# Layer-norm statistics combined by ScalarE and VectorE on 32 partitions instead of by TensorE, in a fused gated cross-attention and feed-forward block

## The chip, the cores and the metric

The kernel runs on one core of one Trainium2 chip. A core has five engines that work side by side, each on its own queue of instructions, in order: PE (TensorE, matmuls; its weight loads are shown as PEld), DVE (VectorE), ACT (ScalarE), POOL (GpSimd) and SP (SyncE, which issues DMAs here). On-chip data lie in SBUF, 128 partitions wide; PE writes its results to PSUM, from where DVE and ACT take them ("evict" them). The metric is the device time of one execution in microseconds; lower is better. Before the change it is 1263.37 us, the median of 3 runs (1262.82 to 1263.95).

## The reference

x is 4 x 2048 x 512, the context 4 x 77 x 384, all in float32. Sixteen heads of width 64. Layer norm has neither gain nor offset.

```python
def _layernorm(x, axis=-1, eps=1e-05):
    m = jnp.mean(x, axis=axis, keepdims=True)
    v = jnp.var(x, axis=axis, keepdims=True)
    return (x - m) / jnp.sqrt(v + eps)
...
    def _L0_xattn_ref(x, context, Wq, Wk, Wv, Wo, bo):
...
        q = split_heads(x @ Wq)
        k = split_heads(context @ Wk)
        v = split_heads(context @ Wv)
        sim = jnp.einsum('bhid,bhjd->bhij', q, k) * SCALE
        attn = jax.nn.softmax(sim, axis=-1)
        out = jnp.einsum('bhij,bhjd->bhid', attn, v)
...
        return out @ Wo + bo

    def _L0_ffn_ref(x, W, b, logits, u):
...
        gumbel = -jnp.log(-jnp.log(u))
        idx = jnp.argmax(jax.nn.log_softmax(logits) + gumbel)
        out = jnp.einsum('btd,de->bte', x, W[idx]) + b[idx]
        return out
    x = x + jnp.tanh(g_xattn[0]) * _L0_xattn_ref(_layernorm(x, axis=-1), ctx_768, ...)
    x = x + jnp.tanh(g_ffn[0]) * _L0_ffn_ref(_layernorm(x, axis=-1), ...)
    return x
```

## The kernel before

**Weights folded into the keys and values.** Since the context is short (77 keys, padded to 80), the kernel multiplies the query weights into the keys once per batch element (`m`, from `build_m`) and the output weights into the values (`vo`, from `build_vo`, which evicts six products per head pair p, by DVE or ACT after a string such as "AAD", and stores them to HBM; `load_vo` and `load_m` fetch what a batch element needs). Scores are then x times `m`, and the attention's output is the probabilities times `vo`. The centring of the layer norm is folded into the weights, so that only its factor, one over the standard deviation, has to be found for each token.

**Tiles.** The 8192 tokens are cut into 16 groups of 512. A group's rows lie in SBUF as 128 partitions x 16 x 128: partition 32a + c holds, for 16 tokens (one for each g), the a-th quarter of their 512 features. A token's statistics are therefore spread over four partitions, 32 apart. `x_columns` transposes the rows to columns for PE.

**Seven products instead of eight.** `Seven` multiplies two by two blocks by a scheme of seven products (the Strassen-Winograd sums T1 to T4 are computed by POOL in `Columns.sum`). `product(s)` issues the matmuls of step s; `post(s)` evicts what is finished: ACT copies a result to `snap`, or DVE adds one to it. Some later products accumulate in a PSUM bank that an earlier `post` must have emptied. There are seven such banks (`bank`), and an eighth, `stat`, is shared by the statistics and by `head_max`.

**Softmax.** `s_rows` (DVE) transposes scores to rows of tokens, `head_max` finds a maximum for each head quarter, `exps` (ACT) computes 64 rows of exponentials per group with the factor `up` and the offset `nmx`, `head_sum` (DVE) sums and inverts, `head_scale` (POOL) multiplies, `p_columns` (DVE) transposes the probabilities back for PE as `pT`.

**Order.** The order of the instructions on every engine is written out by hand (`manual_schedule`): an engine takes its instructions as the program emits them, and semaphores hold it where data are missing. One turn of the main loop, for group i, holds the scores of group i (ps_s, three `Seven`s: s0, then s1 and s2 together), the attention output of group j = i - 1 (ps_a) and its feed-forward product (ps_f), and the residual end of group f = i - 2 (`f_rows`, `f_scale` by ACT, `add_bias` and `f_add` by POOL, `store` by SP). Ahead of the loop, the scores of groups 0 and 1 are interleaved with `build_vo`; behind it stands the rows' end, the rest of groups 14 and 15, where work is cut into halves of 8 token rows.

**The statistics** (`Norms`, lines 361 to 422). A turn treats two norms at once: that of the feed-forward of group f (16 columns, flag `y`) and that of the next scores (16 columns, flag `x`), so n = 32; at the start and the end n is 16 or 8. `stats` runs bn_stats (DVE) for every g: it gives two means and two sums of squares for even and odd features, on each of the four partitions. `mean` adds the two means (L379), and `flush` (L384) multiplies by the constant `jm`, 128 x 128, which is 0.125 where two partitions agree modulo 32: PE thus sums over the four partitions and writes the result back to all of them. `spread` computes the deviations from PSUM (L399, L401, L403), `var` sums again and uses PE again, `rstd` adds epsilon (L412) and raises to the power -0.5 on POOL (L415, L422), 16 columns at a time; `up` and `down` (L418, L419) scale the factor for the exponentials. In the main loop `mean` stands behind s0's last `post`, and the other three steps at s = 1, 2, 3 of the loop over s1 and s2. At the start and the end, with `apart` set, the matmul is emitted one step behind the sums.

**The start and the rows' end.** At the start, `early_step` places norms[0] and norms[1] in the loop over s1 of group 0 (lines 710 to 732). In the loop over s0 of group 1 (756 to 769), `build_vo(4)` to `build_vo(7)` are interleaved with the first 57 rows of exponentials of group 0; the last seven follow at line 770, ahead of the loop over s1 and s2. At the rows' end, group 15's feed-forward is finished in halves: `half_bias` adds the bias, `scaled` (ACT) and line 1063 (DVE) apply the factor, `added` (DVE) adds, and two `store` calls write the halves, by SP and by ACT's queue.

Of the kernel before, what the change touches and what calls it, by code (L numbers as in the profile page):

```python
# [19 lines left out]
def flamingo_block_kernel(  # L20
# [82 lines left out]
    jm = cp.tile([P, NA, 32], F32, tag="jm")  # L103
# [85 lines left out]
    nc.gpsimd.memset(jm, 0.0)  # L189
    for a in range(NA):  # L190

        for a2 in range(NA):
            nc.gpsimd.affine_select(
                out=jm[:, a, :], in_=jm[:, a, :], compare_op=ALU.not_equal, fill=0.125,
                base=-32 * a2, pattern=[[-1, 32]], channel_multiplier=1)
# [165 lines left out]
    class Norms:  # L361


        apart, waiting = False, None

# [11 lines left out]
        def total(self, pairs, half):  # L377
            t = small.tile([P, self.n], F32, tag=f"tot{half}", name="tot")
            nc.vector.tensor_reduce(t, pairs, AX.X, ALU.add)  # L379
            self.waiting = half, t  # L380

        def flush(self):
            half, t = self.waiting
            nc.tensor.matmul(self.ps[:, half], jm.rearrange("p a c -> p (a c)"), t, start=True, stop=True)  # L384

        def mean(self):
            n = self.n
            self.ps = stat[:, : 2 * n].rearrange("p (h n) -> p h n", h=2)
            self.mm = self.s6.rearrange("p g (h s) -> p g h s", h=2)
            self.total(self.mm[:, :, :, 1], 0)  # L390
            if not self.apart:
                self.flush()

        def spread(self):
            n = self.n
            sq = stat[:, ds(4 * NG, 2 * n)].rearrange("p (n h) -> p n h", h=2)
            dv = small.tile([P, n, 2], F32, tag="dv", name="dv")
            for t in (dv, sq):
                nc.vector.tensor_tensor(t, self.mm[:, :, :, 1],  # L399
                                        self.ps[:, 0].unsqueeze(2).to_broadcast([P, n, 2]), ALU.subtract)  # L400
            nc.vector.tensor_tensor(sq, sq, dv, ALU.mult)  # L401
            self.q = small.tile([P, n, 2], F32, tag="q", name="q")
            nc.vector.scalar_tensor_tensor(self.q, self.mm[:, :, :, 2], 1.0 / 64, sq, ALU.mult, ALU.add)  # L403

        def var(self):
            self.total(self.q, 1)
            if not self.apart:
                self.flush()

        def rstd(self):  # L410
            self.rs = small.tile([P, self.n], F32, tag="rs", name="rs")
            nc.vector.tensor_scalar(self.rs, self.ps[:, 1], EPS, None, ALU.add)  # L412
            if self.x:
                r = self.rs[:, ds(self.x0, NG)]
                nc.gpsimd.tensor_tensor(r, r, neghalf, ALU.pow)  # L415
                self.up = small.tile([P, NG], F32, tag="up", name="up")
                self.down = small.tile([P, NG], F32, tag="down", name="down")
                nc.gpsimd.tensor_scalar(self.down, r, -SCALE, None, ALU.mult)  # L418
                nc.gpsimd.tensor_scalar(self.up, r, SCALE, None, ALU.mult)  # L419
            if self.y:  # L420
                r = self.rs[:, : min(self.n, NG)]
                nc.gpsimd.tensor_tensor(r, r, neghalf[:, : min(self.n, NG)], ALU.pow)  # L422
# [117 lines left out]
    def head_max(i, h):  # L540
        mx = stat[:, ds((8 + h) * NG, NG)]
# [132 lines left out]
    def norm_step(n, s):  # L674
        if s < 4:
            (n.mean, n.spread, n.var, n.rstd)[s]()

    def early_step(n, s):

        if s == 0:  # L680
            n.apart = True
            n.mean()
        elif s == 1:
            n.flush()
            n.spread()
            n.var()
        elif s == 2:
            n.flush()
            n.rstd()
# [20 lines left out]
    for s in range(7):  # L710
        s1.product(s)
        if s == 0:
# [3 lines left out]
            early_step(n, 0)  # L716
# [3 lines left out]
        elif s < 3:  # L720
            early_step(n, s)
            n1.stats(xg[1], 0, 8 * (s - 1), 8)
        elif s < 6:
            early_step(n1, s - 3)
        if 0 < s:
            s1.post(s)
        if s == 4:
# [8 lines left out]
    for s in range(7):  # L736
        s2.product(s)
        s2.post(s)
        if s == 5:
# [16 lines left out]
    for s in range(6):  # L756
        s0.product(s)
        s0.post(s)
        if s < 4:
            build_vo(4 + s, "DDA" if s < 2 else "D")  # L760
# [9 lines left out]
    exps(0, 57, 64)  # L770
    for s in range(7):
        s1.product(s)
        s2.product(s)
        if s == 0:
            s1.post(0)
            s2.post(0)
            s0.product(6)
# [24 lines left out]
    for i in range(1, NGRP):  # L802
# [4 lines left out]
        if 1 < i:  # L807

            s0 = scores0(i)
            for s in range(6):  # L810
# [18 lines left out]
                if s == 3 and 0 <= f:  # L829
                    add_bias(f, nc.gpsimd)  # L830
            for k in range(2):
# [4 lines left out]
            for s in range(7):  # L836
                s1.product(s)
                s2.product(s)
                if s == 0:
# [4 lines left out]
                    n.mean()  # L844
                    for k in range(2):
                        s_rows(i, KH + k, s0.chunk(1, k))
                elif s < 4:
                    norm_step(n, s)
# [111 lines left out]
    for s in range(7):  # L960
# [9 lines left out]
        if s == 1:  # L970
            n.apart = True
            n.mean()
            add_bias(f, nc.vector)
        if s == 2:
            n.flush()
            n.spread()
            n.var()
            pT[j].sum("T4")
        if s == 3:
            n.flush()  # L980
            n.rstd()
# [12 lines left out]
        if s == 6:  # L994
# [4 lines left out]
            n1.apart = n0.apart = True  # L999
            n1.mean()  # L1000
# [19 lines left out]
    def added(h, v):  # L1020
        y = by_feature(ys[j], h, v)
        nc.vector.tensor_tensor(y, y, by_feature(ts_[j], h, v), ALU.add)

    for s in range(6):
        ff.product(s)
        if s == 0:
            n1.flush()
            n1.spread()
            n1.var()
            y_rows(j, 2, 0)  # L1030
            n0.stats(ys[j], 0, 0, 8)
        if s == 1:
            n1.flush()
            n1.rstd()
            yc[j].sum("T4")
            n0.mean()
            half_bias(1, nc.vector)
        if s == 2:
            n0.flush()
            half_bias(0, nc.gpsimd)  # L1040
            n0.spread()
# [66 lines left out]
```

## Time and profile before

| | before |
|---|---|
| runs, median | 1263.37 us (1262.82 to 1263.95) |
| profiled execution, its own time | 1261.51 us |
| its span | 1259.6 us |
| TensorE clock granted, mean | 0.998 |
| matmul passes of the 128 x 256 kind, each | 379 ns from start to end, one every 0.216 us |
| statistics matmuls (L384) | 38, recorded as 76 passes |
| pow on POOL, 128 x 16 (L415) | 16, 3135 ns in the mean |
| ACT idle, mean over the periods of the main loop | 36 of 73 us |

The span is from the first to the last instruction that the profiler recorded; the execution's own time holds what lies around it too. An fp32 matmul is recorded as two passes. In a timeline, a line gives the start in us, the length in us (of the whole run of like instructions), the engine, the line of the kernel, the operation, the tile written and those read, the shapes, how many there were, and in brackets the idle time before it and what ended it. The engines' busy times overlap: they are not a sum. A line number such as L504 can be that of a helper that many places call.

### The profile page before, as it was taken

How to read it: one execution, taken by the hardware profiler on the slowest of the kernel's cores; microseconds unless marked ns; L12 is line 12 of the kernel's file. 1: busy time of each engine (PE TensorE's matmuls, PEld its weight loads, DVE VectorE, ACT ScalarE, POOL GpSimd, SP SyncE). 2: the span in 40 equal slices, each digit the busy share in tenths (PEclk: the TensorE clock that was granted, in tenths of full speed). 3: DMA queues.
4: the chain of work that ended last, by engine and by line, in shares of the span. 5: the costliest groups of instructions: out<-in, count | busy, mean ns of one | idle time of the engine just before them, and what ended most of it. 6: DMA issues, size and time to landing. Idle time of an engine off the chain costs nothing.

```text
span 1259.6 us, 16932 instructions
## 1 busy us (share of the span) xinstructions
PE 1246.9 (99%) x5780; PEld 1067.7 (85%) x5780; DVE 886.2 (70%) x1858; ACT 639.1 (51%) x1748; POOL 879.0 (70%) x483
## 2 busy tenths in 40 slices
PE   9999999999999999999999999999999999999996
PEld 6575888888888888888888888888888888888885
DVE  5789876667777676777766767766766787666566
ACT  3539453719265372926446292744628273563813
POOL 5352895866957786676968687675976697575764
PEclk9999999999999999999999999999999999999999
DMA  9766400314014030303106030212304120010102
GB/s 271 291 199 214 114 1 1 68 42 109 1 28 124 1 67 1 68 22 98 32 1 151 1 68 1 46 22 84 67 1 110 42 56 11 2 34 1 34 1 67
DMA packets 95221, 80.28 MB, mean 64 GB/s; under 512 B 3856, under 2 KB 83088, under 8 KB 95136
## 3 DMA queue, kind: packets, MB, share of 16 engines
q1 hardware_dynamic: 92768, 76.74, 24.0%
q10 hardware_dynamic: 1760, 1.34, 0.3%
q8 instruction: 46, 0.75, 0.3%
q0 software_dynamic: 608, 1.13, 0.2%
q14 instruction: 39, 0.32, 0.1%
HBM read 44.07 MB, written 35.13 MB: 63 GB/s over the span
## 4 chain that ended last, share of the span: by engine, by line
PE 96%; DVE 2%; ACT 1%; issue 0%; POOL 0%; DVEq 0%; ACTq 0%
PE ps_s L479 38%; PE ps_a L479 37%; PE ps_f L479 15%; PE ps_kv L274 2%; PE ps_vo L339 2%; PE ps_m L304 2%; PE ps_st L384 0%; ACT t L604 0%; PE ps_w L168 0%; ACT t L1018 0%; DVE s L375 0%; DVE snap L504 0%; POOL rs L422 0%; DVE vo L342 0%; DVE y L430 0%
## 5 line engine op out<-in xcount | busy, mean ns | idle before, releaser
L479 PE MATMUL ps_a<-pT,vo 128*128 128x256 f32 x2240 | 486.7, 379 | 0.0
L479 PEld LDWEIGHTS ps_a<-pT,vo 128*128 128x128 f32 x2240 | 425.5, 190 | 57.8
L550 ACT ACTIVATE s<-s,nmx,up 128x77 f32<-128x77 f32 x1024 | 355.6, 446 | 0.4 <-DVE nmx L544 0.3
L479 PE MATMUL ps_s<-tq,m 128*128 128x256 f32 x1280 | 294.2, 381 | 0.2 <-ACT snap L485 0.2
L450 POOL TENSOR_TENSOR pT<-pT 128x1280 f32<-128x1280 f32 x64 | 185.8, 2904 | 125.3 <-PE ps_a L479 111.7
L479 PEld LDWEIGHTS ps_s<-tq,m 128*128 128x128 f32 x1280 | 241.3, 190 | 35.8 <-issue 3.2
L485 ACT COPY snap<-ps_s 128x512 f32<-128x512 f32 (+1 forms) x188 | 93.8, 511 | 306.8 <-DVE t L430 131.4
L479 PE MATMUL ps_s<-xc,m 128*128 128x256 f32 x960 | 222.7, 381 | 0.0
L479 PEld LDWEIGHTS ps_s<-xc,m 128*128 128x128 f32 x960 | 180.8, 190 | 28.2 <-DVE vo L342 2.4
L561 POOL TENSOR_TENSOR s<-s,sm 128x1232 f32<-128x1232 f32 x64 | 145.1, 2268 | 65.9 <-DVE sm L558 46.1
L504 DVE TENSOR_TENSOR snap<-snap,ps_s 128x512 f32<-128x512 f32 (+1 forms) x141 | 83.5, 593 | 82.0 <-PE ps_s L479 82.0
L533 DVE STREAM_TRANSPOSE s<-snap 128x512 f32<-128x512 f32 x156 | 99.9, 685 | 46.8 <-ACT snap L485 44.8
L604 ACT ACTIVATE t<-t,rs 128x128 f32<-128x128 f32 x240 | 73.3, 389 | 100.7 <-POOL rs L422 100.7
L479 PE MATMUL ps_f<-tq,wf 128*128 128x256 f32 x512 | 118.7, 379 | 0.0
L570 DVE STREAM_TRANSPOSE pT<-s 128x512 f32<-128x512 f32 x160 | 101.0, 677 | 17.1 <-POOL s L561 17.1
L415 POOL TENSOR_TENSOR rs<-rs,neghalf 128x16 f32<-128x16 f32 x16 | 50.2, 3135 | 87.9 <-DVE rs L412 87.9
L450 POOL TENSOR_TENSOR tq<-xc,tq 128x512 f32<-128x512 f32 x64 | 85.2, 1332 | 34.9 <-PE ps_f L479 32.4
L479 PEld LDWEIGHTS ps_f<-tq,wf 128*128 128x128 f32 x512 | 97.0, 190 | 13.1
L557 DVE TENSOR_REDUCE sm<-s 128x16 f32<-128x1232 f32 x64 | 91.4, 1429 | 20.5 <-ACT s L550 20.5
L542 DVE TENSOR_REDUCE ps_st<-s 128x16 f32<-128x1232 f32 x64 | 92.4, 1444 | 2.1
L479 PE MATMUL ps_f<-xc,wf 128*128 128x256 f32 x384 | 90.8, 379 | 0.0
L450 POOL TENSOR_TENSOR tq<-xc 128x512 f32<-128x512 f32 x64 | 81.4, 1271 | 10.7 <-DVE xc L425 9.4
(126 smaller groups left out, 1137.7 us busy)
## 6 DMA issues: line engine op xcount, KB each, us to landing
xg<-in_x_dram SPq DMA_DIRECT2D x64, 256.0 KB, 5.8
out_dram<-y SPq DMA_DIRECT2D x60, 256.0 KB, 4.3
vo<-vo_d SPq DMA_DIRECT2D x16, 640.0 KB, 6.5
vo_d<-vo SPq DMA_DIRECT2D x16, 512.0 KB, 4.3
m<-m_d SPq DMA_DIRECT2D x12, 640.0 KB, 4.2
m_d<-vo SPq DMA_DIRECT2D x4, 960.0 KB, 7.9
wq<-in_WqT_dram SPq DMA_DIRECT2D x8, 256.0 KB, 6.5
wq<-in_Wo_dram SPq DMA_DIRECT2D x1, 2048.0 KB, 13.8
```

Of the source, the lines that this page charges most:

```text
L415: nc.gpsimd.tensor_tensor(r, r, neghalf, ALU.pow)
L450: (engine or nc.gpsimd).tensor_tensor(self.at[name], self.at[a], self.at[b_], op)
L479: nc.tensor.matmul(self.ps[r][:, n, :], self.w(blk, c, pair), self.cols(cname, c), start=(first and n == 0 and c == 0), stop=(c == h - 1), ...
L485: nc.scalar.copy(dst, self.ps[r])
L504: nc.vector.tensor_tensor(c, c, self.ps[r], ALU.add)
L533: nc.vector.transpose(key_chunk(sc[i], k), cols.rearrange("p (g h r) -> p g h r", h=HA, r=R))
L542: nc.vector.tensor_reduce(mx, head(i, h), AX.X, ALU.max)
L550: nc.scalar.activation(head(i, h)[:, g, :], head(i, h)[:, g, :], AF.Exp, scale=norms[i].up[:, g : g + 1], bias=nmx[h][:, g : g + 1])
L557: nc.vector.tensor_reduce(sm, head(i, h), AX.X, ALU.add)
L561: nc.gpsimd.tensor_tensor(head(i, h), head(i, h), sums[h].unsqueeze(2).to_broadcast([P, NG, J]), ALU.mult)
L570: nc.vector.transpose(pT[i].all[:, k, :].rearrange("p (g h r) -> p g h r", h=HA, r=R), key_chunk(sc[i], k))
L604: nc.scalar.activation(ts_[f][:, g, :], ts_[f][:, g, :], AF.Copy, scale=rs[:, g : g + 1])
```

## The change

In the place of `mean`, `spread`, `var`, `rstd` and the constant `jm` there are four other steps, and no matmul. `gather`: eight ACT copies bring the two means and the two sums of squares of the four partition quarters side by side on 32 partitions, the means to PSUM (`stat`), the sums to SBUF. `calc`: seven DVE operations on 32 partitions x n x 8 give the variance. `power`: POOL raises to -0.5, on 32 partitions, 16 columns at a time. `back`: four copies (by ACT, once by DVE) bring the factor to all 128 partitions; POOL then computes `down` and `up`. `head_max` moves to another part of `stat`.

Where the steps stand: in the main loop `gather` behind s0's loop, ahead of the first evictions of s1 and s2, `calc` and `power` at s = 0, `back` at s = 3. At the start, norms[0] takes s = 0, 1 and 3 of the loop over s1, and norms[1] s = 3 of that loop (`gather`) and s = 0 and 3 of the loop over s2. In the loop with `build_vo`, `build_vo(7)` is evicted as "DDA" instead of "D", so that its third and sixth product go to ACT. The last seven exponentials of group 0 come behind the first evictions of s1 and s2. At the rows' end both bias halves go to POOL, the scaling of the quarter (0, 0) and two of the four additions too, and the half that is stored first is finished after the last product instead of before it.

```diff
     class Norms:
...
-        def mean(self):
...
-        def spread(self):
...
-        def var(self):
...
-        def rstd(self):
+        def gather(self):
+
+            self.mean = stat[:32, : 8 * self.n].rearrange("p (n e) -> p n e", e=2 * NA)
+            self.m2 = small.tile([32, self.n, 2 * NA], F32, tag="m2", name="m2")
+            parts = self.s6.rearrange("p g (h s) -> p g h s", h=2)
+            for a in range(NA):
+                for to, k in ((self.mean, 1), (self.m2, 2)):
+                    nc.scalar.copy(to[:, :, ts(a, 2)], parts[ts(a, 32), :, :, k])
+
+        def calc(self):
...
+            tot, dv, self.r = tile_of([], "tot"), tile_of([2 * NA], "dv"), tile_of([], "r32")
+            nc.vector.tensor_reduce(tot, self.mean, AX.X, ALU.add)
+            wide = tot.unsqueeze(2).to_broadcast([32, self.n, 2 * NA])
+            for to in (dv, self.mean):
+                nc.vector.scalar_tensor_tensor(to, wide, -0.125, self.mean, ALU.mult, ALU.add)
+            nc.vector.tensor_tensor(self.mean, self.mean, dv, ALU.mult)
+            nc.vector.scalar_tensor_tensor(dv, self.m2, 1.0 / 64, self.mean, ALU.mult, ALU.add)
+            nc.vector.tensor_reduce(tot, dv, AX.X, ALU.add)
+            nc.vector.tensor_scalar(self.r, tot, 0.125, EPS, ALU.mult, ALU.add)
+
+        def power(self):
+            for at in range(0, self.n, NG):
+                r = self.r[:, at : min(at + NG, self.n)]
+                nc.gpsimd.tensor_tensor(r, r, neghalf[:32, : r.shape[1]], ALU.pow)
+
+        def back(self, copy=nc.scalar.copy):
             self.rs = small.tile([P, self.n], F32, tag="rs", name="rs")
+            for a in range(NA):
+                copy(self.rs[ts(a, 32)], self.r)
             if self.x:
                 r = self.rs[:, ds(self.x0, NG)]
-                nc.gpsimd.tensor_tensor(r, r, neghalf, ALU.pow)
...
     def norm_step(n, s):
-        if s < 4:
-            (n.mean, n.spread, n.var, n.rstd)[s]()
...
         if s == 0:
+            n.gather()
         elif s == 1:
+            n.calc()
+            n.power()
         elif s == 2:
+            n.back()
...
+        if s == 0:
+            norm_step(n1, 1)
+        if s == 3:
+            norm_step(n1, 2)
...
         if s < 4:
-            build_vo(4 + s, "DDA" if s < 2 else "D")
+            build_vo(4 + s, "D" if s == 2 else "DDA")
...
-    exps(0, 57, 64)
     for s in range(7):
         s1.product(s)
         s2.product(s)
         if s == 0:
             s1.post(0)
             s2.post(0)
+            exps(0, 57, 64)
             s0.product(6)
             s0.post(6)
...
+            n.gather()
             for k in range(2):
                 s_rows(i, k, s0.chunk(0, k))
...
                     s0.product(6)
                     s0.post(6)
-                    n.mean()
+                    n.calc()
+                    n.power()
                     for k in range(2):
                         s_rows(i, KH + k, s0.chunk(1, k))
-                elif s < 4:
-                    norm_step(n, s)
+                elif s == 3:
+                    n.back()
...
     for s in range(6):
         ff.product(s)
         if s == 0:
+            half_bias(1, nc.gpsimd)
+            n1.calc()
+            n1.power()
             y_rows(j, 2, 0)
             n0.stats(ys[j], 0, 0, 8)
             yc[j].sum("T4")
+            half_bias(0, nc.gpsimd)
+        ff.post(s)
         if s == 2:
+            n1.back()
+            n0.gather()
         if s == 3:
             f_rows(j, ff, 0, 1)
             scaled(0, 1, n1.rs)
+            n0.calc()
+            n0.power()
         if s == 4:
             f_rows(j, ff, 1, 1)
             scaled(1, 1, n1.rs)
+            added(0, 1, nc.gpsimd)
         if s == 5:
             f_rows(j, ff, 0, 0)
+            n0.back(nc.vector.tensor_copy)
+            scaled_at_once(0, 0, n0.rs, nc.gpsimd)
+            added(0, 0, nc.gpsimd)
     ff.product(6)
     for k in range(2):
         to_rows(ts_[j], ff.ps[0][:, k, :], 2 + k, 0)
+    added(1, 1, nc.vector)
+    store(j, 8, 8, (nc.sync, nc.sync, nc.sync, nc.scalar))
+    scaled_at_once(1, 0, n0.rs, nc.vector)
+    added(1, 0, nc.vector)
     store(j, 0, 8, (nc.sync, nc.scalar))
```

## The prediction

> **What bounds the kernel now.** I read the busy shares first, then the chain that ended last, then TensorE's timeline in one period of the main loop, then the timelines of all engines at the start and at the end.
>
> ```profile
> PE 1246.9 (99%) x5780; PEld 1067.7 (85%) x5780; DVE 886.2 (70%) x1858; ACT 639.1 (51%) x1748; POOL 879.0 (70%) x483
> PE 96%; DVE 2%; ACT 1%; issue 0%; POOL 0%; DVEq 0%; ACTq 0%
> ```
>
> PE is 99% busy and makes 96% of the chain: what leaves PE leaves the time, and what the other engines do is free until PE waits for it. That gives three questions: what the removed matmuls cost on PE, where the new work makes PE wait, and what becomes of the stretch after PE's last matmul.
>
> ```profile
> 488.80 1.89 PE L479 MATMUL ps_s<-tq,m 128*128 128x256 f32 x8
> 490.52 0.30 PE L384 MATMUL ps_st<-tot,jm 128*128 128x32 f32 x2
> 490.67 5.43 PE L479 MATMUL ps_s<-tq,m 128*128 128x256 f32 x24
> 495.93 0.30 PE L384 MATMUL ps_st<-tot,jm 128*128 128x32 f32 x2
> 496.07 2.84 PE L479 MATMUL ps_s<-xc,m 128*128 128x256 f32 x12
> ```
>
> A line is start, length, group. An fp32 matmul is two passes; in the chain 140 ps_a passes take 30.22 us, 0.2159 each. The first statistics matmul holds PE from 490.52 to 490.67 (0.15), and the 24 passes behind it take 5.26 where 24 x 0.2159 is 5.18 (0.08 more): 0.23 each, and PE waits for nothing here.
>
> **Part 1: the statistics matmuls of the main loop go.** The 14 periods from the first ps_a of one group to that of the next (141.72 to 1163.60) sum to 1021.88 us. A period holds 168 tiled matmuls, 336 passes, 72.53 us; 14 of them 1015.4. So 6.5 us are something else; three periods are 0.12 longer than the others for a reason of their own, which I leave in. Gain **6.1 us**, bounds 4.1 (28 x 0.145, the visible slots alone) and 6.5.
>
> The work that takes their place must hide. One group, in times of before:
> - gather, eight ACT copies: the last bn_stats ends at 485.2, so about 485.2 to 486.6. ACT is idle from 481.8 to 488.5, where s1's first eviction starts.
> - calc, seven VectorE operations, now on 32x256 instead of 128x64: 128x256 rows take 0.42 (L504) to 0.48 (L583), together some 2.7. VectorE is idle from 488.56 to 491.40, so it ends near 491.1; the s_rows behind it wait for ACT until 491.4 anyway.
> - power, two pows of 2.9 (L415) on POOL, idle from 489.8: 491.1 to 497.0, where it was 496.5 to 502.9.
> - back, four ACT copies behind evictions that end at 496.5: 497.0 to 497.7; POOL's down and up to 498.3. Behind them stand f_scale (ready 5 us earlier than before), ACT's evictions at 505.9, and on POOL T2 of pT at 511. None is reached.
>
> So nothing is lost there. If the cover were gone, PE would first feel it at s1's T2 product (493), which needs the eviction behind gather: it has 4 us to spare.
>
> **Part 2: prices of the small operations.** ACT copies of 16 to 64 elements out of SBUF are not in the trace. In the nearest rows, 128x8 and 128x80, ACT starts one 0.12 after the other (48.40, 48.52), or 0.22 where it needs the result (48.18, 48.40). Each PSUM copy of gather waits for the one before: four pairs of 0.24 and a tail, **1.2 us**; back 4 x 0.12 and a tail, **0.6**. Upper bounds at f_scale's pitch (3.03 for 10): 2.4 and 1.2. I take the lower, whose sizes are nearer. calc on 32x128 lies between 128x64 (0.23) and 128x256 (0.42): **2.0**, bounds 1.3 and 2.7. pow with 16 columns: **2.9** as L415, whose columns are the same; bounds 1.65 (L422, 8 columns, the faster) and 4.1 (the longest L415).
>
> The rows just named price the small ACT operation at 0.12 to 0.22. [...]
>
> **Part 3: the start, where cover ends.**
>
> ```profile
> 116.49 1.72 PE L339 MATMUL ps_vo<-wq,wf 64*64 64x512 f32 x4 [0.55 <-DVE snap L504]
> 111.37 13.82 ACT L550 ACTIVATE s<-s,nmx,up 128x77 f32<-128x77 f32 x40
> 128.42 2.26 POOL L561 TENSOR_TENSOR s<-s,sm 128x1232 f32<-128x1232 f32 x1
> 130.72 4.27 DVE L570 STREAM_TRANSPOSE pT<-s 128x512 f32<-128x512 f32 x7 [3.78 <-POOL s L561]
> 137.62 0.64 DVE L504 TENSOR_TENSOR sn<-sn,ps_s 128x512 f32<-128x512 f32 x1
> ```
>
> Lines of PE, ACT, POOL and DVE: ACT computes exponentials without a gap to 125.2; VectorE sums the last head, POOL scales it (to 130.7), VectorE transposes p_columns, and only then adds the score quarter (137.62 to 138.26) that PE's last s1 product needs at 138.97. The slack is 0.7 us, and the change puts work into this chain at two places.
>
> First, norms[1]. Its gather is covered (ACT waits until 85.8 for wfr anyway). Its calc stands on VectorE behind four s_rows: 90.7 to 92.7; pow to 95.6; back to 96.2. ACT's last s2 eviction, now behind back, ends at 96.6 instead of 94.9, and head_max starts at 97.3 instead of 95.7. VectorE is 1.6 late, but had waited 0.57 and 0.67 for PE in this stretch: 0.4 remain. ACT is 0.9 late.
>
> Second, the shifted evictions. Before, ACT had 32 exponentials done at 114.1; now at 115.0 it finds the third and the sixth eviction of build_vo(7). The sixth product is not there before 118.2: PE gets its bank only when VectorE has evicted another, as the first line shows. ACT stands still, evicts, and is free at 118.9. 25 exponentials x 0.345 reach 127.5, the two evictions moved ahead 128.4, the last seven 130.9: 5.7 later. Sum (1.7) and scale (2.26) end at 134.9 instead of 130.7; POOL's own queue had hidden 1.5. All of VectorE's p_columns move by 4.2, the needed add ends at 142.5, and PE, due at 138.97, loses 3.5. The next exponentials start 0.7 later against PE, whose T1 of yc had 0.4 of slack (ready 173.25, needed 173.67): 0.2 more. That swallows what leaves PE before (four statistics matmuls, waits of 0.20 and 0.71). Loss **3.7 us**. Lower bound 3.3 (ACT waits for the sixth product even if norms[1] costs nothing); upper 8.2, with the upper prices of part 2 in all six steps (ACT and VectorE then carry norms[0] late into norms[1] too). jm's 16 selects (0.21 each) leave POOL before 10 us, where PE waits for no POOL: 0.
>
> **Part 4: the rows' end.**
>
> ```profile
> 1231.58 2.29 DVE L608 TENSOR_TENSOR y<-y,t 128x2048 f32<-128x2048 f32 x1 [2.92 <-ACT t L604]
> 1252.95 1.29 DVE L1022 TENSOR_TENSOR y<-y,t 128x512 f32<-128x512 f32 x2
> 1254.28 0.89 ACTq L612 DMA_DIRECT2D out_dram<-y  x2
> ```
>
> The second to last group's pow is free to start when POOL's T4 ends (1221.7, not 1223.8): back at 1225.2, 16 f_scale to 1230.0, f_add to 1232.3 instead of 1233.9. Everything queued behind that add on VectorE is 1.5 earlier: n1's stats end at 1235.9, gather 1237.1, calc 1238.8, n0's stats 1241.1. PE loses six statistics matmuls and a wait of 0.34 and ends near 1248.1, not 1250.2. Then in a row on VectorE: back to 1249.0, two transposes to 1249.8, three adds and scalings of 0.65 to 1251.8. POOL's half: pow to 1248.4, add, scale, add of 1.27 each (L576) to 1252.2. The last store is issued at 1252.1 instead of 1254.3; its issue count per queue and its 5.3 us to the end stay. Gain **2.2**, bounds 1.2 (pow and POOL late) and 2.6.
>
> **Sum.** -6.1 + 3.7 - 2.2 = -4.6: the profiled execution goes from its span of 1259.6 to 1255.0. It ran 1261.5 with what lies around the span, 1.9 under the runs' median of 1263.37, from which the same 4.6 leads to **1258.8**.
>
> **Rivals.**
> - The start gives no loss: PE's last s1 product does not wait, if the add is not what holds it. Against: slack of 0.7 and 13.8 us of unbroken exponentials. -6.1 - 2.2 = 1255.1.
> - The start costs twice as much, through the upper prices: -6.1 + 8.2 - 1.5 = +0.6, so 1264.0, within the measurement. For it: all steps of norms[1] are serial over four engines; against: the nearest ACT rows.
> - Slower: the 0.23 us beside each statistics matmul belong to the change of stage at s1, not to the matmul, and remain. Then the loop gains 0, the start costs 3.7 and the end brings 1.2: 1265.9. It decides only where the loop's gain is about nil. Against: the 0.15 lies between two products of the same stage. With the start beyond 11 us it would come out slower as well.
>
> **How the numbers follow.** Less than 0.2%, 2.5 us, cannot be told from no change. Forecast (1257 to 1261) 0.60; no loss at the start 0.14; doubled 0.16; slower 0.10. Faster: the first two, 0.74, and a little off for the forecast's upper edge: 0.72; same 0.18; slower 0.10. The range reaches from the rival below, 1255.5, to near the doubled start, 1263.3.
>
> **What would show it.** Periods of 72.6 in the main loop and no PE wait there; a PE wait of some 3 us for VectorE's add before the first ps_a; exponentials of group 0 ending near 131; the last store issued 48.1 us after the last group's first ps_a, not 50.3. The forecast is wrong if PE waits in the periods, or if the start's wait is under 2 or over 6.

## The result and the profile after

The changed kernel takes 1262.82 us (median of 12 runs, 1261.32 to 1263.36). The kernel before, run beside it on the same chip, takes 1263.14 (12 runs, 1261.80 to 1264.04). The ratio is 0.9996, 95% interval 0.9987 to 1.0005: no change that can be told. 1258.8 was forecast. The profiled execution has a span of 1261.1 us.

From the page of the changed kernel, TensorE's busy line and the chain that ended last:

```profile
PE 1241.8 (98%) x5704; PEld 1060.5 (84%) x5704; DVE 915.6 (73%) x1857; ACT 686.3 (54%) x1966; POOL 876.8 (70%) x470
PE 94%; DVE 3%; ACT 2%; POOL 0%; issue 0%; DVEq 0%; POOLq 0%; ACTq 0%
```

TensorE has 76 passes (the 38 statistics matmuls) and 5.1 us of work less, as foreseen, but its part of the chain fell from 96% to 94%: VectorE and ACT hold 5% of it now, where it was 3%. Work left TensorE and waits came in. Where, a table from TensorE's timelines tells, with marks that every kernel of this study has: the first ps_kv pass, the first VO product, the first ps_a pass, the first ps_a pass of the loop's last round, and the end of the span (starts of groups of matmuls, us; the 141.72 and 1163.60 of the prediction are two of these marks, 0.16 later by another view).

| kernel | first ps_kv | first VO product | from there to the first ps_a: start | 14 rounds: loop | rows' end | span |
|---|---|---|---|---|---|---|
| before | 5.57 | 51.54 | 90.02 | 1021.88 | 96.16 | 1259.6 |
| before, once more | 5.68 | 51.67 | 90.01 | 1021.87 | 96.15 | 1259.7 |
| changed | 6.22 | 53.21 | 96.60 | 1015.63 | 95.66 | 1261.1 |
| e1: vo(7) back | 5.96 | 53.32 | 91.55 | 1016.05 | 95.68 | 1256.6 |
| e2: and exponentials back | 6.23 | 53.22 | 91.36 | 1015.64 | 95.68 | 1255.9 |
| e3: fillers | 6.47 | 52.44 | 94.93 | 1016.12 | 95.71 | 1259.2 |
| e4: jm made again | 6.59 | 53.59 | 96.67 | 1015.76 | 95.68 | 1261.7 |
| e5: e2, other tail | 6.73 | 53.90 | 91.35 | 1015.64 | 94.91 | 1255.8 |
| e6: e2, norms[1] later | 6.60 | 53.60 | 91.64 | 1015.62 | 95.64 | 1256.5 |
| e8: before, loop alone | 5.57 | 51.62 | 90.02 | 1015.63 | 96.13 | 1253.4 |
| e10: e12, other tail, PSUM | 5.76 | 52.10 | 90.02 | 1015.72 | 94.76 | 1252.6 |
| e11: e6, back at the end | 5.96 | 52.97 | 89.70 | 1016.15 | 95.68 | 1254.5 |
| e12: e8, changed rows' end | 6.73 | 53.80 | 90.01 | 1015.63 | 95.66 | 1255.1 |
| e14: e10, z on GpSimd | 6.36 | 52.34 | 90.01 | 1015.63 | 94.92 | 1252.9 |

From before to changed: start +6.58, loop -6.25, rows' end -0.50, together -0.17 us; the first 52 us, +1.67, belong to the execution and not to the change (see e4, e9 and e12). The three stretches agree with the medians, which differ by -0.32. Kernels whose code is the same in a stretch differ there by 0.16 us at most (rows' end of e10 and e14), most by less than 0.1.

The main loop went as forecast. TensorE's timeline around the second scores, in one round of the changed kernel (start, length, group; in brackets the idle time before it and what ended it):

```profile
487.49 1.89 PE L461 MATMUL ps_s<-xc,m 128*128 128x256 f32 x8
489.22 1.89 PE L461 MATMUL ps_s<-tq,m 128*128 128x256 f32 x8
490.94 4.48 PE L461 MATMUL ps_s<-xc,m 128*128 128x256 f32 x20
```

No ps_st group stands between them, and no line has a bracket: TensorE waits for nothing here. Between 90 and 150 us it waits four times:

```profile
91.69 1.13 PE L461 MATMUL ps_s<-tq,m 128*128 128x256 f32 x4 [1.46 <-ACT snap L467]
104.98 1.97 PE L461 MATMUL ps_s<-tq,m 128*128 128x256 f32 x8 [0.82 <-DVE vo L334]
119.48 1.72 PE L331 MATMUL ps_vo<-wq,wf 64*64 64x512 f32 x4 [0.55 <-DVE snap L486]
145.43 4.54 PE L461 MATMUL ps_s<-tq,m 128*128 128x256 f32 x12 [3.31 <-DVE sn L486]
```

Of these only the third was there before. The chain that ends in the fourth, from the timelines of ACT, POOL and VectorE in the changed kernel:

```profile
118.97 0.69 ACT L336 ACTIVATE vo<-ps_vo,tg 128x512 f32<-128x512 f32 x1 [1.77 <-PE ps_vo L331]
121.24 0.68 ACT L336 ACTIVATE vo<-ps_vo,tg 64x512 f32<-64x512 f32 x1 [1.59 <-PE ps_vo L331]
121.83 8.65 ACT L532 ACTIVATE s<-s,nmx,up 128x77 f32<-128x77 f32 x25
...
131.12 2.51 ACT L532 ACTIVATE s<-s,nmx,up 128x77 f32<-128x77 f32 x7
...
135.53 2.27 POOL L543 TENSOR_TENSOR s<-s,sm 128x1232 f32<-128x1232 f32 x1 [2.73 <-DVE sm L540]
...
137.82 4.27 DVE L552 STREAM_TRANSPOSE pT<-s 128x512 f32<-128x512 f32 x7 [2.44 <-POOL s L543]
...
144.72 0.65 DVE L486 TENSOR_TENSOR sn<-sn,ps_s 128x512 f32<-128x512 f32 x1
```

ACT waits for the third and for the sixth product of vo(7), as the prediction said, and every link behind it is late. What the prediction had not is the last figure of the fourth PE line: twelve passes take 4.54 us (4.38 to the first ps_a pass) where twelve of 0.216 are 2.6. The busy times by microsecond of the changed kernel (window, length, then busy PE, PEld, DVE, ACT, POOL; the number after POOL is the granted clock of TensorE) show why:

```profile
144.00:145.00 1.00, 0.00 (x0) 0.00 (x0) 1.00 (x3) 0.00 (x0) 1.00 (x1) 1.00 0.00 0
145.00:146.00 1.00, 0.57 (x2) 0.49 (x3) 1.00 (x3) 0.00 (x0) 1.00 (x1) 0.81 0.00 0
146.00:147.00 1.00, 1.00 (x4) 0.81 (x3) 1.00 (x3) 0.00 (x0) 0.92 (x2) 0.50 0.00 0
147.00:148.00 1.00, 1.00 (x4) 0.72 (x4) 1.00 (x2) 0.00 (x0) 1.00 (x1) 0.50 0.00 0
148.00:149.00 1.00, 1.00 (x4) 0.81 (x3) 1.00 (x4) 0.00 (x0) 1.00 (x1) 0.50 0.00 0
149.00:150.00 1.00, 1.00 (x6) 0.90 (x5) 1.00 (x3) 0.59 (x1) 0.92 (x2) 0.98 0.03 8
```

After the wait the clock is 0.50 for three microseconds, each with four passes begun or under way where six are usual. The wait of 3.31 us costs more than itself. Behind the shorter waits at 91.69 and 104.98 the granted clock stays at 1.00.

### The profile page after: what moved, and what is told of

Same layout as the page of the kernel before. It is cut to its first block, busy times and chain, and to the rows that moved or that the text cites. A ratio compares the mean times of both kernels' runs of the same rounds, so it can differ in the third digit from the quotient of the medians.

```text
span 1261.1 us, 16981 instructions
## 1 busy us (share of the span) xinstructions
PE 1241.8 (98%) x5704; PEld 1060.5 (84%) x5704; DVE 915.6 (73%) x1857; ACT 686.3 (54%) x1966; POOL 876.8 (70%) x470
## 3 DMA queue, kind: packets, MB, share of 16 engines
q10 hardware_dynamic: 1760, 1.34, 0.3%
## 4 chain that ended last, share of the span: by engine, by line
PE 94%; DVE 3%; ACT 2%; POOL 0%; issue 0%; DVEq 0%; POOLq 0%; ACTq 0%
PE ps_a L461 38%; PE ps_s L461 36%; PE ps_f L461 15%; PE ps_kv L266 2%; PE ps_vo L331 1%; PE ps_m L296 1%; ACT s L532 1%; DVE pT L552 0%; PE ps_w L167 0%; DVE vo L334 0%; DVE snap L486 0%; ACT wf L644 0%; ACT snap L467 0%; DVE t L412 0%; DVE z L219 0%
## 5 line engine op out<-in xcount | busy, mean ns | idle before, releaser
L393 POOL TENSOR_TENSOR r<-r,neghalf 32x16 f32<-32x16 f32 (+1 forms) x33 | 93.1, 2832 | 25.8 <-DVE r L388 25.2
L467 ACT COPY snap<-ps_f 128x512 f32<-128x512 f32 x63 | 36.9, 586 | 89.1 <-PE ps_f L461 89.1
```

Of the source, the lines that this page charges most:

```text
L393: nc.gpsimd.tensor_tensor(r, r, neghalf[:32, : r.shape[1]], ALU.pow)
L467: nc.scalar.copy(dst, self.ps[r])
```

## The experiments

All were run with five rounds beside the kernel before (e9 with one). Ratios are to it, with 95% intervals; its median was 1263.07 in the first job (e1 to e4), 1262.96 in the second (e5, e6, e8, e9) and 1263.71 in the third. The intervals reach 1.1 to 1.7 us to either side, so smaller steps between two variants rest on the stretches of the profiles, not on the times. "Start" and "rows' end" are columns of the table. Rows' end runs from the first ps_a pass of the loop's last round, which the expectations call the last group's.

### e1 and e2: the shifted evictions and exponentials, undone

```
-            build_vo(4 + s, "D" if s == 2 else "DDA")
+            build_vo(4 + s, "DDA" if s < 2 else "D")
```

> The changed kernel with the evictions of vo(7) as before (all six by VectorE; ACT keeps four of vo(4) and vo(5) only). Theory A, that the 2.0 to 2.5 us of vo(7)'s products on ACT and ACT's waits for them (1.77 and 1.59 us) push the last exponentials of group 0 past the cover of the PE stream, and that the 3.31 us wait of TensorE on line 486 and the slow passes behind it (4.54 for 2.6 us) follow from that: the last exponentials end 4 to 5 us earlier, the wait before the T4 passes is under 0.5 us, the twelve passes take 2.6 us, the stretch from the first VO product to the first ps_a pass is 91.0 to 92.5 us (96.59 in the changed kernel, 90.01 before), the time about 1257.5 to 1258.5. Rival B, that the delay is already there when the new statistics chain ends (98.4 us) and the evictions only fill it: the stretch stays at 95 or more, and the time at 1261.5 to 1263.

e2 has this and the exponentials where they were:

```
+    exps(0, 57, 64)
     for s in range(7):
...
-            exps(0, 57, 64)
```

> As the run before, and the last seven exponentials of group 0 again issued ahead of the snapshots of the next scores. Theory A: the shift of the exponentials is worth little by itself, since seven exponentials at 0.3 us lie on either side of the same snapshots: the stretch is within 1.5 us of the run with vo(7) alone, on either side. Rival C, that the exponentials put behind the snapshots are the larger part of the late start: the stretch falls by 2 us or more against that run.

e1: 1258.62 us, ratio 0.9966 (0.9954 to 0.9978). The start is 91.55, 5.05 us shorter than in the changed kernel and inside the forecast; neither the wait of 3.31 nor the slow passes are left. The last exponentials end at 130.37, 3.4 us earlier after the first VO product and not 4 to 5, and the time is 0.1 above the 1257.5 to 1258.5 expected. e2: 1258.32, 0.9962 (0.9948 to 0.9975); start 91.36. So vo(7)'s evictions cost 5.05 us and the place of the seven exponentials 0.19. Theory A holds, rivals B and C fall. In e1, 0.42 of the 5.05 are given back in the loop's first round (72.94 us for 72.52), where TensorE waits 0.15 us at 177.12 for a sum of GpSimd (tq); in e2 it doesn't.

### e3: TensorE kept busy in the wait

```
+            for k in range(16):
+                nc.tensor.matmul(stat[:, 320:448], ones, ones, start=True, stop=True)
```

Put behind the snapshots of step 5, ahead of s1.product(6).

> The changed kernel with sixteen 128x128 products of the constant tile, of no use, on TensorE in the gap ahead of the T4 passes, into 128 columns of the statistics bank that nobody reads. Theory A, that the twelve T4 passes took 4.54 us because the granted clock fell to about 0.5 after 3.3 us without work: the fillers take some 3 us of the gap, the passes start as late as before (within 0.5 us) and take 2.6 to 2.9 us, the clock stays over 0.9 there, and the time falls by 1.7 to 2.0 us to about 1261. Rival D, that the passes were slow from their operands (ports, late data) or that the clock falls anyway: they take 4 us or more, time unchanged.

TensorE's timeline, and the clock in the same microseconds, in the kernel with fillers:

```profile
141.21 3.73 PE L775 MATMUL ps_st<-ones 128*128 128x128 f32 x32
144.78 2.76 PE L461 MATMUL ps_s<-tq,m 128*128 128x256 f32 x12
147.37 0.81 PE L461 MATMUL ps_a<-pT,vo 128*128 128x256 f32 x3
```

```profile
144.00:145.00 1.00, 1.00 (x11) 0.97 (x10) 1.00 (x4) 0.00 (x0) 1.00 (x1) 1.00 0.00 0
145.00:146.00 1.00, 1.00 (x6) 0.90 (x5) 1.00 (x2) 0.00 (x0) 1.00 (x1) 1.00 0.00 0
146.00:147.00 1.00, 1.00 (x7) 0.87 (x6) 1.00 (x3) 0.29 (x1) 0.92 (x2) 1.00 0.00 0
```

The passes start 92.34 us after the first VO product (92.22 in the changed kernel), so nothing upstream moved, and they take 2.59 us to the first ps_a pass instead of 4.38. The clock stays at 1.00. The start is 1.67 shorter. Work of no use is worth 1.7 us in this stretch, since it keeps the clock. The time, 1261.85 (0.9992; 0.9983 to 1.0001), is 1.0 under the changed kernel's 1262.82 (0.5 by the ratios) rather than 1.7 to 2.0, and the intervals overlap. Of the 1.67, 0.48 are given back in the loop's first round, where TensorE waits 0.22 us at 179.69 for the same sum of GpSimd as in e1. Theory A holds for the passes and the clock, D falls; a gain in the whole time is not shown. How long the clock stays down can be estimated from the windows of the changed kernel: if it steps between 1.00 and 0.50, the 0.81 and the 0.98 above put it at 0.50 from about 145.6 to 149.0, 3.4 us. The wait ahead of it is shown as 3.31 us; counted from 141.96, where the next pass would have started, it is 3.47. From what length on a wait lowers the clock, these runs do not show: behind 1.46 us it stayed at 1.00, behind 3.31 us it fell.

### e4 and e9: the first 52 us

e4 makes the old constant tile again, unread, to give GpSimd its sixteen selects back.

```
+    nc.gpsimd.memset(jm, 0.0)
+    for a in range(NA):
+        for a2 in range(NA):
+            nc.gpsimd.affine_select(out=jm[:, a, :], in_=jm[:, a, :], compare_op=ALU.not_equal, fill=0.125,
+                                    base=-32 * a2, pattern=[[-1, 32]], channel_multiplier=1)
```

> The changed kernel with the constant tile that the old statistics used made again on GpSimd at the start (one memset and sixteen selects; nobody reads it). Theory E, that its removal lets GpSimd reach the sum on line 123 some us earlier, so that it runs beside VectorE's z (2.96 us instead of 0.23) and holds the m products 0.7 us and the first VO product 1.0 us late: z takes about 0.23 us, the first VO product starts at 51.7 to 52.5 us (53.38 in the changed kernel, 51.71 before), and the time falls by 1.0. Rival F, that this is a difference from run to run or comes from the transfers: z stays long in this kernel, or the other kernels of this job, whose start is the changed kernel's, have a short z; the time stays.

e9 is the kernel before, unchanged.

> The kernel before once more, for a second profile of its first 55 us. Theory M, that whether VectorE's z meets GpSimd's sum on line 131 differs from execution to execution, and that the profiled execution of before (1261.5 us, below its median of 1263.1) was one without the meeting: this profile may show z at 2.9 us and the first VO product at 52.4 to 53.6 us, with a span 1 to 2 us longer than 1259.6. Rival N, that the first 52 us belong to the kernel: z 0.23 us and the first VO product at 51.7 again, within 0.3.

e4: 1263.49 (1.0001; 0.9992 to 1.0011), z (VectorE's small subtraction for the gates) again 2.97 us, the first VO product at 53.59: theory E falls. e9: 1262.89, z 0.23, first VO product at 51.67. This looked like rival N, that the early stretch belongs to the kernel; e12, whose code for the first 52 us is that of the kernel before with jm and all, speaks against it. VectorE's and POOL's timelines in e12:

```profile
43.12 2.98 DVE L227 TENSOR_SCALAR z<-lg,st 128x8 f32<-128x8 f32 x1
...
43.19 2.89 POOL L124 TENSOR_TENSOR m<-m 128x1280 f32<-128x1280 f32 x1
```

and in the profile of before:

```profile
41.89 0.23 DVE L227 TENSOR_SCALAR z<-lg,st 128x8 f32<-128x8 f32 x1
...
42.02 2.90 POOL L124 TENSOR_TENSOR m<-m 128x1280 f32<-128x1280 f32 x1
```

The same instructions start 0.07 us apart in the one and 0.13 in the other; in the first, z ends with GpSimd's sum. e3 and e10 have 0.07 as well and a z of 0.23. Each start has so been seen with both lengths: that of before in e12 (long), e8 and e10 (short), that of the changed kernel in e3 (short) and all others (long). So it differs by execution, on a margin finer than these starts resolve, and a long z goes with 1.0 us to the first VO product (46.0 to 46.3 us from the first ps_kv pass without, 47.0 to 47.4 with). The rest of the spread lies ahead of the first ps_kv pass (5.57 to 6.73), where the first weights are still being loaded (5.6 to 6.6 us in the median from issue to landing, in before, e9 and changed); its cause stays open. The spans of before reach from 1259.6 to 1262.4 over the runs of this study, and both of its profiles are from the low end. Theory M agrees with all this; no one kernel was profiled in both forms.

### e8 and e12: the loop alone, and rows' end with it

e8 is the kernel before with the new statistics for norms[2] to norms[15] only.

```
-            norms[nx] = Norms(nx)
+            norms[nx] = Quick(nx)
...
+            n.gather()
             for k in range(2):
                 s_rows(i, k, s0.chunk(0, k))
...
-                    n.mean()
+                    n.calc()
+                    n.power()
...
-                elif s < 4:
-                    norm_step(n, s)
+                elif s == 3:
+                    n.back()
```

Quick is the changed kernel's class, and head_max's columns of the bank move as there.

> The kernel before with the new statistics for the fourteen norms of the main loop alone; start and rows' end as before, PE statistics there too. Theory A: the main loop is 6.1 to 6.4 us shorter by itself (14 periods; 1021.9 before, 1015.6 in the changed kernel), the start is as before, the time about 1256.7 to 1257.2, ratio 0.995. Rival L, that the loop's gain needs the changed start (which buffers are free, what is late) or is given back at rows' end: 1259 or more.

e8: 1255.90 us, 0.9952 (0.9938 to 0.9965). Loop 1015.63, to the hundredth that of the changed kernel; start 90.02 and rows' end 96.13 those of before. The loop's 6.25 us need nothing of the rest. The time is 0.8 under the 1256.7 expected, with five runs from 1255.11 to 1258.90. Theory A holds, rival L falls.

e12 takes over the changed kernel's rows' end too.

> The kernel before with the new statistics in the main loop and the changed kernel's rows' end, order and all; start as before, with PE statistics for the first two groups. Theory A: rows' end is worth 0.5 us by itself, as the two traces say (96.0 us before and 95.5 changed from the last group's first ps_a pass): span 0.3 to 0.9 us below the run with the loop alone for the same first 52 us, time about 1255.4. Rival O, that the 2.2 us of the prediction are there and were hidden in the changed kernel by what its start left late: 1.5 us or more below the run with the loop alone.

e12: 1256.55, 0.9945 (0.9931 to 0.9958). Rows' end 95.66 against 96.13: 0.47 us, where the prediction had 2.2. The time is above the 1255.4 expected, in a job where before is 0.75 slower, and the first VO product of the profiled execution is 2.18 later than in e8; from there to the end of the span it takes 1201.3 against 1201.8. Theory A holds, O falls.

### e5 and e10: what holds rows' end

In the changed kernel VectorE's scalar operation on line 388 and its last product are long. Timelines of VectorE and POOL:

```profile
1221.33 2.59 DVE L388 TENSOR_SCALAR r<-tot 32x16 f32<-32x16 f32 x1
...
1221.00 2.89 POOL L432 TENSOR_TENSOR pT<-pT 128x1280 f32<-128x1280 f32 x1 [4.11 <-PE ps_a L461]
...
1252.42 0.93 DVE L1004 TENSOR_TENSOR y<-y,t 128x512 f32<-128x512 f32 x1
1253.28 1.75 DVE L1000 TENSOR_TENSOR t<-t,rs 128x512 f32<-128x512 f32 x1
1255.06 0.69 DVE L1004 TENSOR_TENSOR y<-y,t 128x512 f32<-128x512 f32 x1
...
1252.89 1.59 POOL L1004 TENSOR_TENSOR y<-y,t 128x512 f32<-128x512 f32 x1
```

Sixteen columns take 2.59 us, to the end of POOL's T4 (1223.89), and the product that took 0.69 before (line 1063 there) takes 1.75 beside POOL's sum. e5 is e2 with the tail dealt out otherwise:

```
-            scaled_at_once(0, 0, n0.rs, nc.gpsimd)
-            added(0, 0, nc.gpsimd)
+            scaled(0, 0, n0.rs)
+            added(1, 1, nc.gpsimd)
...
-    added(1, 1, nc.vector)
     store(j, 8, 8, (nc.sync, nc.sync, nc.sync, nc.scalar))
     scaled_at_once(1, 0, n0.rs, nc.vector)
+    added(0, 0, nc.vector)
     added(1, 0, nc.vector)
```

> The run with vo(7) and the exponentials restored, and the last additions and products of rows' end dealt out anew: the product of quarter (0,0) by ACT, the sum of quarter (1,1) by GpSimd, the sums of (0,0) and (1,0) by VectorE, so that no two-input operation of VectorE runs beside GpSimd after the last transposes. Theory G, that VectorE's last product (1.75 us; 0.69 before) and the sum ahead of it (0.93) were long because GpSimd's sum of (0,0) ran beside them: both take 0.65 to 0.75 us again, the last sum ends 0.5 to 0.7 us earlier against the last TensorE pass, time 0.5 to 0.7 us lower than with vo(7) and the exponentials restored (1258.3). Rival H, that the product is long from its broadcast operand or from its tile: it stays over 1.5 us.

VectorE's last product in e5:

```profile
1247.99 0.92 DVE L1000 TENSOR_TENSOR t<-t,rs 128x512 f32<-128x512 f32 x1
```

e5: 1256.79, 0.9950 (0.9936 to 0.9963), 1.5 under e2 where 0.5 to 0.7 were expected. Rows' end 94.91 against 95.68: 0.77, which is the new dealing out as a whole. The product takes 0.92 and not 0.65 to 0.75; in e10, which has the same tail and a product of 0.93, the first 0.38 of it still lies beside a sum of POOL (1244.05 to 1245.31). The sums take 0.65 each. Theory G holds in the main, rival H falls.

e10 is e12 with this tail and one operand moved:

```
+            tot = stat[:32, ds(20 * NG, self.n)]
             nc.vector.tensor_reduce(tot, dv, AX.X, ALU.add)
             nc.vector.tensor_scalar(self.r, tot, 0.125, EPS, ALU.mult, ALU.add)
```

> As the run with loop and rows' end, with the last additions dealt out anew (GpSimd the sum of quarter (1,1), ACT the product of (0,0), VectorE the sums of (0,0) and (1,0)) and the last total of the calculation in PSUM in place of SBUF. Theory G: VectorE's scalar operation on line 388 (2.59 and 0.62 us beside a running GpSimd operation, 0.16 alone) has an operand outside SBUF then and doesn't wait: 0.15 to 0.25 us in all calls; rows' end is 0.7 to 1.8 us shorter than with the changed kernel's; time 1253.6 to 1254.8, the shortest of all. Rival P, that the scalar operation waits for GpSimd all the same, since it writes SBUF: 2.6 and 0.6 us again, and only the 0.7 us of the additions are gained.

The same place, VectorE and POOL, in e10:

```profile
1213.75 0.16 DVE L448 TENSOR_SCALAR r<-ps_st 32x16 f32<-32x16 f32 x1
...
1213.41 2.89 POOL L492 TENSOR_TENSOR pT<-pT 128x1280 f32<-128x1280 f32 x1 [4.08 <-PE ps_a L521]
```

POOL's T4 runs as before beside it, and the scalar operation no longer waits: 0.15 to 0.18 us in all 17 calls. Theory G holds, P falls. Rows' end is 94.76, 0.9 shorter than in e12; time 1255.66, 0.9940 (0.9926 to 0.9953), above the 1253.6 to 1254.8 expected, like e12 in the same job. e5 had 0.77 of the 0.9 from the tail alone, so the freed scalar operation is worth 0.1 at most, less than the 0.16 between e10 and e14, whose rows' end is the same: POOL's pow stands behind T4 anyway (it starts at 1216.26, when T4 ends). Why the two engines hold each other up, no run here shows. Shown are the lengths: beside the same T4 the scalar operation takes 2.59 us with its source in SBUF (changed kernel) and 0.16 with it in PSUM (e10), and VectorE's last product takes 1.75 beside POOL's sum (changed kernel), 0.92 in e5, and 0.69 in before, where POOL is idle at that time.

### e6 and e11: the copies of norms[1] in ACT's queue

After e2 the start was still 1.34 us longer than before. In the changed kernel, ACT's copies of norms[1]'s back wait for the pow ahead of a snapshot:

```profile
97.55 0.84 ACT L398 COPY rs<-r 32x16 f32<-32x16 f32 x4 [4.32 <-POOL r L393]
```

e6 is e2 with norms[1]'s steps later:

```
         if s == 3:
             norm_step(n, 2)
-            norm_step(n1, 0)
...
-        if s == 0:
-            norm_step(n1, 1)
         if s == 3:
-            norm_step(n1, 2)
+            norm_step(n1, 0)
...
     exps(0, 57, 64)
+    n1.calc()
...
             head_scale(0, 3)
+            n1.power()
...
         if s == 2:
+            n1.back()
             pT[0].sum("T1")
```

> The run with vo(7) and the exponentials restored, and the statistics of the second group taken later, where nobody waits for them: gather behind a snapshot of the third scores, the calculation behind the sum of the third head, the power behind GpSimd's last product of group 0. Theory I, that the rest of the late start (91.4 us against 90.0 before) is ACT's queue: the copies that gather and bring back norms[1] hold the last snapshots of the second and third scores, so that TensorE waits 1.5 us at 91.7 and 0.8 us at 105.0: both waits fall under 0.4 us, the stretch from the first VO product to the first ps_a pass is 89.0 to 90.2 us, time 1256.2 to 1257.5. Rival K, that the chain of the first group's statistics (gather, calculation, power, back) sets it, or that the work moved later stops VectorE or GpSimd ahead of the first ps_a pass: the stretch stays at 91 or more, time 1258 or more.

e6: 1257.68, 0.9958 (0.9944 to 0.9971). The wait at 105 is gone and that at 91.7 fell to 0.95, but the start is 91.64. ACT's and TensorE's timelines show a new wait:

```profile
135.85 0.85 ACT L398 COPY rs<-r 32x16 f32<-32x16 f32 x4 [5.02 <-POOL r L393]
136.72 0.58 ACT L467 COPY sn<-ps_s 128x512 f32<-128x512 f32 x1
...
137.36 2.86 PE L461 MATMUL ps_s<-tq,m 128*128 128x256 f32 x12 [1.76 <-ACT sn L467]
```

The four copies of back stand in ACT's queue ahead of a snapshot, wait 5 us for the pow, and TensorE waits for the snapshot. So the mechanism that e6 was to remove had only been moved. e11 puts back behind the last snapshot:

```
-        if s == 2:
-            n1.back()
...
+    n1.back()
     for sv, k0, nk in ((s1, 2, 2), (s2, 4, 1)):
```

> The run with the second group's statistics later, and their copies back to 128 partitions put behind the last snapshots of the next scores. Theory I: the 1.76 us wait of TensorE at 137.4 came from those copies, which stood in ACT's queue ahead of a snapshot and waited for GpSimd; it is gone, the stretch from the first VO product to the first ps_a pass falls from 91.6 to 89.6 to 90.2 us, and the time by 1.4 to 2.0 to about 1256. Rival Q, that the calculation moved into VectorE's queue made the wait: a wait of over 1 us remains, the stretch stays over 91.

e11: 1256.27, 0.9944 (0.9931 to 0.9958). Start 89.70: 1.66 under e2 and 0.32 under before. The wait at 137.4 is gone; the 0.95 at 91 remains. Theory I holds and Q falls. Rival K had e6's start (over 91) but not its cause: the queue was ACT's, not VectorE's or GpSimd's, and between e6 and e11 the place of back alone is worth 1.94. Of e11's gain 0.5 us are given back in the loop's first round (73.03 us for 72.52), where TensorE waits 0.24 us at 175.02 for GpSimd's tq, as in e1 and e3.

### e14: z out of VectorE's queue

```
-        nc.vector.tensor_scalar(z, lg, st[:, 0:1], None, ALU.subtract)
+        nc.gpsimd.tensor_scalar(z, lg, st[:, 0:1], None, ALU.subtract)
...
-    weight_sum(m, 0)
     build_m(2, 0, 2, stages[2:], NP // 2)
     gates0()
+    weight_sum(m, 0)
```

> As the run with the last additions dealt out anew, and z of the gates computed by GpSimd, ahead of its sum on line 124, in place of VectorE beside it. Theory M, that in a part of the executions of every kernel here VectorE's z starts within 0.1 us of GpSimd's sum and then waits it out, which makes the first VO product some 1.0 us late: no execution has the wait, the spans of this kernel lie within 1.0 us of one another, and the median is 0.3 to 1.0 us below the run without this step. Rival R, that the spread of the spans (1259.6 to 1262.4 before) has another source: it stays at 2 us, the median within 0.3.

e14: 1254.90 us, 0.9932 (0.9919 to 0.9946), the shortest measured, 0.76 under e10. Its five spans lie within 1.1 us (1252.5 to 1253.6), 0.1 more than expected, and e10's within 2.0. With five runs each this agrees with theory M and doesn't prove it. e11's start with e14's rest was not tried.

## Why the prediction was off

- **Part 1, the main loop: right.** -6.25 us for the forecast 6.1, within bounds of 4.1 and 6.5, without a wait, and e8 has the whole of it alone. The rival that the 0.23 beside each matmul would remain fell.
- **Part 2, the prices: low.** gather takes 1.6 us (85.97 to 87.58 for norms[1]; forecast 1.2), back 0.84 (0.6), calc 1.9 (2.0), pow 2.9 as forecast. gather's four pairs of copies start 0.38 to 0.47 apart, where 0.24 was priced, and back's four copies take 0.21 each, where 0.12 was.
- **Part 3, the start: the mechanism right, the size not.** Forecast +3.7, measured +6.58. The step "the needed add ends at 142.5, and PE, due at 138.97, loses 3.5" came out: in before's time (1.67 earlier) the add ended at 143.7, and TensorE was due at 140.3 (139.37 and twelve passes of 0.216, less 1.67), 3.4 apart (3.5 to the pass that then starts). Two terms stood at nothing. TensorE itself is 1.3 late there: norms[1] was given "ACT is 0.9 late" and no wait of TensorE, while TensorE waits 1.46 at 91.69, which uses up what left it, and 0.82 at 104.98. And a wait of 3.3 us was priced at its length; the slow clock behind it adds 1.8 (4.38 for 2.59 us; 1.67 by e3). 1.3 + 3.5 + 1.8 make the 6.6. By experiments: vo(7) 5.05 (the clock's loss among it), exponentials 0.19, the place of norms[1]'s four steps 1.66 (e2 against e11), the rest -0.32.
- **Part 4, rows' end: off.** Forecast -2.2, measured -0.50 (e12: -0.47). Two steps failed. "PE loses six statistics matmuls and a wait of 0.34 and ends near 1248.1, not 1250.2" makes 1.7 by the prediction's own prices (six of 0.23, and 0.34), not 2.1; TensorE's last pass ends 1.34 earlier against the mark where rows' end begins, with a new wait of 0.37 before its last product. And "three adds and scalings of 0.65 to 1251.8" took each operation at its length without POOL: line 1004 takes 0.93 and line 1000 1.75, since the new order puts POOL's product and sum beside them, and VectorE ends 4.9 us behind TensorE's last pass for a forecast of 3.7. The last stores are issued 49.8 us after the last group's first ps_a, where 48.1 was the sign and 50.3 is before's.
- **Sum.** -6.25 + 6.58 - 0.50 = -0.17 for -4.6. The loop's gain went into the start. The measured 1262.82 lies outside the forecast's 1257 to 1261 and just inside the wide range, whose upper end stands for the rival of a start that costs twice. That rival had the size nearly (1264.0), by luck: from prices of 2.4 us for gather, where 1.6 was measured, and not from the clock.
- **jm at nothing: right** (e4). That executions of this kernel differ by some 2 us the prediction could have read from the 1.9 us between its profile and its median, though not that they do so in the first 52 us.

## What to carry to other kernels

An operation that waits belongs behind everything in its engine's queue that somebody else needs: the same four copies cost 1.9 us ahead of a snapshot (e6) and nothing that shows behind it (e11). A wait of TensorE as long as the 3.31 us here has to be priced with the slow passes behind it (4.38 us for 2.59); waits of 1.46 and 0.82 brought none. Before giving GpSimd a share of a tail, look at what VectorE does in the same microsecond (its last product took 1.75 us beside POOL's sum, 0.69 with POOL idle) and where its operands lie (2.59 us with the source in SBUF, 0.16 in PSUM); and where a change has several parts, run its best part alone, which here (e8) was worth 0.5% against nothing for the whole.

## What had not been expected of the hardware

- The granted clock falls to 0.50 after a wait of 3.31 us and comes back some 3.6 us after work has begun (145.43 to about 149.0, estimated from the windows): 1.7 to 1.8 us lost on twelve passes.
- A VectorE scalar operation on 16 columns takes 2.59 us beside a GpSimd sum (changed kernel) and 0.16 beside the same sum when its source is in PSUM (e10).
- Starting first in the trace doesn't protect VectorE: z, shown 0.05 to 0.07 us ahead of GpSimd's sum, waited for the whole of it in eight of the thirteen profiles that have z on VectorE; in e3 and e10, 0.07 ahead, it didn't, nor in three that show it 0.08 to 0.33 ahead.
